# A graph layer on one core: other sizes of the last node blocks, narrower ranges for the last chunks, and row loads every 76 gathers up to near the end

## The chip, the cores and the metric

The kernel runs on one core of a Trainium2 chip. A core has five engines, each with its own queue of instructions: TensorE (PE; loads of weights are listed apart, as PEld), VectorE (DVE), ScalarE (ACT), GpSimd (POOL) and SyncE (SP, which here does nothing but start transfers). The time is that of the device from start to end of the launch, in microseconds (us); lower is better.

## What is computed

One layer of a graph network over 12,500 nodes of 128 features and 200,000 edges. `dst` is sorted, `src` is not.

```python
h = jnp.maximum(_layernorm(x, axis=-1), 0.0)
msgs = h[src]
agg = jax.ops.segment_sum(msgs, dst, num_segments=n)
deg = jax.ops.segment_sum(jnp.ones((src.shape[0],)), dst, num_segments=n)
agg = agg / jnp.maximum(deg, 1.0)[:, None]
g = jax.nn.relu(agg @ Wg + h @ Ws + bg)
g = jnp.tanh(g @ W1 + b1)
g = jnp.tanh(g @ W2 + b2)
out = x + g @ W3 + b3
```

Wg and Ws are 128x128, W1 128x512, W2 512x512, W3 512x128. All is float32.

## The kernel before

**Chunks.** The edges are cut into 1563 chunks of 128 edges. Since `dst` is sorted, a chunk's destinations lie in a short range of nodes: `window(c)` (L97) gives its first node and its width from `WINDOWS` (L49), 144 nodes for most chunks, 88 from chunk 1496, 56 from chunk 1536. A chunk takes one matmul: its 128 source rows are the weights, and a one-hot matrix (edge by node of the range) streams, so that sums per node arise in PSUM, features on the partitions. The one-hots are made by DVE for eight chunks at a time (`onehot`, L349), with a sum over the eight (`cnt`) from which `count` (L379) takes the nodes' degrees.

**Where rows come from.** There are three ways to fetch the 128 source rows of a chunk:

- 80 raw chunks (`raw`, L80) take rows of x before the layer norm, by 80 gathers on POOL during the set-up, and are normed later.
- Most chunks take one gather on POOL from the table `htab` of normed rows in DRAM (`gather`, L297), at most `AHEAD` = 32 gathers ahead of the chunk that is being added.
- The chunks of the list `slow` (L84) are fetched row by row by SP, with 128 transfers of 512 bytes (`row_loads`, L314). Their addresses are loaded in the set-up (`at_i`, one transfer a chunk on ACT's queue; `place`, one DVE instruction). The list begins at chunk `SLOW0` = 160 and then takes a chunk after each `EACH` chunks that are not raw. The rows are loaded in batches of `LOADS` = 16; eight batches, spread over about `EACH` gathers, fill one of two buffers (L637).

**Blocks.** The nodes are cut into blocks (L104): 23 of 512, then 256, 128, 128, 128 and the remaining 84. `reach` lists the chunks whose range touches a block; chunks that touch two blocks are summed into a bank of their own, `edge`, and `merge` (L438) adds that to both. When the last of a block's chunks is added, and two more chunks (`lead`, L648, in the last part), the block is merged and its layers begin: `part0` multiplies by the reciprocal degree (`mT`, DVE), then ws and wg; `part1` to `part3` are the three dense layers, with an ACT step after each product; `part4` turns the result back by TensorE transposes and adds x.

**Order.** TensorE's instructions stand in an order written out by the main loop (L616): chunk by chunk, with steps of the layers in between. From chunk `QUICK` = 1376 on, a small plan of due times (`there`, L642, and `costs`, L493) decides which layer steps go between two chunks. SP's transfers stand in program order as well: loads of own rows (`hb`), of x (`xb`, `xs`), the batches of row loads, and stores of results. POOL does nothing but gathers.

At the end the kernel sums the degrees; if an edge fell outside its range, they don't add up to 200,000, and a second, general way computes all again (`flag`, L674).

Of the kernel before, what the change touches and what calls it, by code (L numbers as in the profile page):

```python
# [31 lines left out]
P = 128  # L32
EPS = 1e-5
CPR = 16
BLK = 512
# [4 lines left out]
STEP = 40  # L40
AHEAD = 32
SLOW0 = 160
EACH = 80
LOADS = 16
LATE = 12
LEAD = 10
QUICK = 1376

WINDOWS = ((0, 144), (1496, 88), (1536, 56))  # L49
W_RAW = 160  # L50
W_MAX = max(W_RAW, *(w for _, w in WINDOWS))

# [6 lines left out]
def windowed(ctx, tc, x, src, dst, Wg, Ws, bg, W1, b1, W2, b2, W3, b3, out, flag):  # L59
    nc = tc.nc  # L60
    N, D = x.shape
# [9 lines left out]
    NCH = -(-E // P)  # L71
# [4 lines left out]
    assert D == P and H % P == 0 and per * E == N * P and RAW0 % GRP == STEP % GRP == 0  # L76
    assert all(c % GRP == 0 for c, _ in WINDOWS) and RAW1 <= WINDOWS[1][0]


    def raw(c):  # L80
        return RAW0 <= c < RAW1 and (c - RAW0) % STEP < GRP


    slow, n = [], 0  # L84
    for c in range(SLOW0, NCH - 100):
        if not raw(c):
            if n == 0:
                slow.append(c)
                n = EACH
            else:  # L90
                n -= 1


    def first(w, span=per):
        return (span - w) // 2

    def window(c):  # L97
        if raw(c):
            return per * (c - c % GRP) + first(W_RAW, per * GRP), W_RAW
        w = [w for c0, w in WINDOWS if c0 <= c][-1]  # L100
        return per * c + first(w), w

    blocks, n = [], 0
    for w in [BLK] * (N // BLK - 1) + [BLK // 2] + [P] * 3:  # L104
        blocks.append((n, w))
        n += w
    blocks.append((n, N - n))

    dram = ctx.enter_context(tc.tile_pool(name="dram", bufs=1, space=bass.MemoryType.DRAM))
    const = ctx.enter_context(tc.tile_pool(name="const", bufs=1))  # L110
# [24 lines left out]
    q_i = const.tile([P, CPR], I32, name="q_i")  # L135
    nc.gpsimd.iota(q_i, pattern=[[per, CPR]], base=first(WINDOWS[0][1]), channel_multiplier=0)

# [47 lines left out]
    with tc.tile_pool(name="setup", bufs=1) as sp, tc.tile_pool(name="ln", bufs=2) as ln:  # L185
# [58 lines left out]
        )  # L244
        for c0, w in WINDOWS[1:]:
            v = low[:, c0:]
# [3 lines left out]
        nc.vector.scalar_tensor_tensor(  # L250
            steps[:, :, :GRP], rdst, float(first(WINDOWS[0][1]) - first(W_RAW, per * GRP)),
            at[:, :, :1].to_broadcast([P, NRAW, GRP]), op0=ALU.add, op1=ALU.subtract,
# [118 lines left out]
    for c in range(NCH):  # L371
        lo, w = window(c)
# [243 lines left out]
    for c in range(NCH):  # L616
# [18 lines left out]
        if not raw(c) and c not in slow:  # L635
            behind += 1
            batch = behind * P // (EACH * LOADS)  # L637
            if behind > SLOW0 - 2 * EACH and batch > (behind - 1) * P // (EACH * LOADS):
                next(loading, 0)
# [366 lines left out]
@with_exitstack  # L1006
def gnn_kernel(ctx: ExitStack, tc: tile.TileContext, *args):
    nc = tc.nc
    keep = ctx.enter_context(tc.tile_pool(name="flags", bufs=1))
    flag = keep.tile([1, 1], I32, name="flag")  # L1010
    with ExitStack() as inner:
        windowed(inner, tc, *args, flag)
    outside = nc.values_load(flag, min_val=0, max_val=P)
    with tc.If(outside > 0):
        with ExitStack() as inner:
            general(inner, tc, *args)
# [31 lines left out]
```

## Time and profile before

| | us |
|---|---|
| median of 3 runs | 1957.18 (1956.88 to 1958.13) |
| the profiled execution, its time | 1961.69 |
| the profiled execution, its span | 1959.5 |
| POOL: 80 raw gathers | 77.4 busy, first part of the span |
| POOL: 1467 gathers from `htab` | 1387.6 busy, started from 104.7 to 1938.6 |
| PE busy | 1393.8 |
| DVE busy | 1068.2 |
| mean granted clock of TensorE | 0.901 |

A page of the profile has the busy time of each engine, the chain of work that ended last (followed back from the last instruction to what released it), and the costliest groups of instructions: source line, engine, operation, what is written from what, count, busy time, mean duration in ns, and the idle time just before them with what ended it. "issue" is time in which an engine waited for nothing that the profile shows. A timeline lists instructions in order; a table by stages has the busy time of each engine in a stretch of the span, and the share of full speed that TensorE's clock was granted in it. TensorE's float32 products appear as two passes each, so "x2" is one matmul. Numbers such as L299 are lines of the kernel before.

### The profile page before, as it was taken

The page shows a single profiled execution, that of the slowest core. Times are in us where ns is not written, and L with a number is a line of the kernel's source. Part 1 is how long each engine was busy: PE and PEld are TensorE (multiplying, and loading weights), DVE is VectorE, ACT ScalarE, POOL GpSimd, SP SyncE. Part 2 cuts the span into 40 slices and gives each one's busy share as a digit, 9 for nine tenths or more (in the row PEclk, how much of TensorE's full clock was granted, in tenths as well). Part 3 has the DMA queues.
Part 4 walks back from the last instruction along what each step waited for, and adds up shares of the span by engine and source line. Part 5 has one row for each costly group of instructions (what it writes and reads, how often), then busy time and mean ns, then how long its engine had stood idle before and what let it go on. Part 6 is the DMA issues. An engine that isn't in the chain of part 4 may idle for free.

```text
span 1959.5 us, 19291 instructions
## 1 busy us (share of the span) xinstructions
PE 1393.8 (71%) x5213; PEld 824.1 (42%) x5213; DVE 1068.2 (55%) x650; ACT 231.8 (12%) x364; POOL 1465.9 (75%) x1555
## 2 busy tenths in 40 slices
PE   0056677777788778877777777777677677778897
PEld 0034344444454445533443434444343333454566
DVE  6974775555667656645545545455454554545430
ACT  1100211011111111010110110110001101101122
POOL 7777777777777777777777777777777777777774
PEclk9999778899989998899989888889889898879697
DMA  7822222222222222222222222222222222222221
GB/s 195 232 69 64 54 64 65 59 70 69 59 65 70 66 74 54 70 70 53 71 59 65 69 53 70 65 59 70 59 65 64 60 70 59 71 69 69 56 61 40
DMA packets 123684, 139.31 MB, mean 71 GB/s; under 512 B 32558, under 2 KB 97978, under 8 KB 123372
## 3 DMA queue, kind: packets, MB, share of 16 engines
q0 software_dynamic: 49504, 101.48, 20.4%
q1 hardware_dynamic: 70870, 33.19, 6.2%
q10 hardware_dynamic: 3192, 3.32, 0.6%
q8 instruction: 43, 0.70, 0.2%
q14 instruction: 75, 0.61, 0.1%
HBM read 125.05 MB, written 12.82 MB: 70 GB/s over the span
## 4 chain that ended last, share of the span: by engine, by line
DMA 36%; issue 28%; PE 26%; POOL 7%; DVE 3%; ACT 0%; SPq 0%; ACTq 0%; POOLq 0%; DVEq 0%
DMA rows<-htab,scol 34%; PE pm L286 13%; PE agg L286 9%; POOL rows L299 7%; PE edge L286 3%; DMA xt<-in_x_dram 2%; PE pt L289 1%; DMA at_i<-in_src_dram 0%; DVE oh L357 0%; DVE agg L176 0%; DVE h L183 0%; DVE agg L172 0%; DVE xt L173 0%; DVE cnt L367 0%; DVE shared L176 0%
## 5 line engine op out<-in xcount | busy, mean ns | idle before, releaser
L299 POOL DMA_INDIRECT rows<-htab,scol x1467 | 1387.6, 946 | 447.5 <-issue 269.3
L286 PE MATMUL agg<-oh,rows 128*128 128x144 f32 (+3 forms) x2096 | 560.2, 365 | 335.2 <-DMA rows<-htab,scol 324.3
L286 PEld LDWEIGHTS agg<-oh,rows 128*128 128x128 f32 x2096 | 381.9, 223 | 714.1 <-DMA rows<-htab,scol 597.5
L286 PE MATMUL pm<-h,w 128*128 128x512 f32 (+3 forms) x1344 | 639.0, 573 | 1.1 <-ACT h L515 0.7
L357 DVE TENSOR_TENSOR oh<-shared,dloc 128x1152 f32<-128x1152 f32 (+2 forms) x186 | 243.9, 1318 | 542.0 <-PE agg L286 330.6
L367 DVE TENSOR_REDUCE cnt<-oh 128x200 bf16<-128x1600 f32 (+2 forms) x186 | 524.3, 2824 | 4.6
L286 PE MATMUL edge<-oh,rows 128*128 128x144 f32 (+2 forms) x838 | 212.2, 346 | 124.3 <-DMA rows<-htab,scol 123.8
L286 PEld LDWEIGHTS edge<-oh,rows 128*128 128x128 f32 x838 | 145.0, 210 | 277.1 <-DMA rows<-htab,scol 242.3
L286 PEld LDWEIGHTS pm<-h,w 128*128 128x128 f32 x1344 | 219.8, 202 | 15.2 <-issue 12.0
L540 ACT ACTIVATE h<-pm,b2c 128x512 f32<-128x512 f32 (+3 forms) x112 | 70.9, 633 | 554.8 <-PE pm L286 554.8
L527 ACT ACTIVATE h<-pm,b1c 128x512 f32<-128x512 f32 (+3 forms) x112 | 70.5, 633 | 237.4 <-PE pm L286 236.9
L142 POOL DMA_INDIRECT raw<-in_x_dram,rsrc x80 | 77.4, 967 | 25.5 <-issue 23.8
L394 DVE RECIPROCAL rd<-rd 128x512 f32<-128x512 f32 (+3 forms) x28 | 81.8, 2920 | 0.0
L564 DVE TENSOR_TENSOR o<-pt,xb 128x512 f32<-128x512 f32 x23 | 15.9, 690 | 95.7 <-PE pt L289 91.9
L508 DVE TENSOR_TENSOR mT<-agg,rd 128x512 f32<-128x512 f32 (+3 forms) x28 | 17.4, 620 | 86.6 <-PE agg L286 86.6
L201 PE MATMUL pm<-ident,idx_f 98*128 98x98 f32 x32 | 6.2, 376 | 64.2 <-DVE idx_f L197 57.8
L392 DVE TENSOR_SCALAR rd<-pm 128x512 f32<-128x512 f32 (+3 forms) x28 | 17.4, 622 | 61.6 <-PE pm L286 61.6
L515 ACT ACTIVATE h<-pm,bgc 128x512 f32<-128x512 f32 (+3 forms) x28 | 17.7, 633 | 271.8 <-PE pm L286 271.8
L472 ACT COPY hT<-pt 128x512 f32<-128x512 f32 (+1 forms) x25 | 14.4, 578 | 258.5 <-PE pt L289 246.9
L286 PE MATMUL pm<-hT,ws 128*128 128x512 f32 (+3 forms) x56 | 41.2, 831 | 0.0
L550 ACT ACTIVATE h<-pm,b3c 128x512 f32<-128x512 f32 (+3 forms) x28 | 17.7, 633 | 181.9 <-PE pm L286 181.9
L289 PE MATMUL pt<-ident,hb 128*128 128x128 f32 x98 | 16.6, 297 | 31.5 <-DMA srows<-htab 31.5
(69 smaller groups left out, 499.1 us busy)
## 6 DMA issues: line engine op xcount, KB each, us to landing
srows<-htab SPq DMA_DIRECT2D x2048, 0.5 KB
rows<-htab,scol POOLq DMA_INDIRECT x1467, 2.5
hb<-htab SPq DMA_DIRECT2D x24, 256.0 KB
xb<-in_x_dram SPq DMA_DIRECT2D x23, 256.0 KB
out_dram<-o SPq DMA_DIRECT2D x23, 256.0 KB
htab<-h SPq DMA_DIRECT2D x6, 896.0 KB
xt<-in_x_dram SPq DMA_DIRECT2D x5, 896.0 KB
raw<-in_x_dram,rsrc POOLq DMA_INDIRECT x80, 3.9
```

The source lines that it names most:

```text
L142: nc.gpsimd.indirect_dma_start(out=t[:, j, :], out_offset=None, in_=x, in_offset=bass.IndirectOffsetOnAxis(ap=rsrc[:, g, j : j + 1], axis=0),)
L286: tc.keep_in_program_order(nc.tensor.matmul(*a, **k))
L289: tc.keep_in_program_order(nc.tensor.transpose(*a, **k))
L299: nc.gpsimd.indirect_dma_start(out=r, out_offset=None, in_=htab, in_offset=bass.IndirectOffsetOnAxis(ap=scol[:, c : c + 1], axis=0),)
L357: nc.vector.tensor_tensor(oh[:, :k, :w], lane[:, None, :w].to_broadcast([P, k, w]), dloc[:, g * GRP : g * GRP + k][:, :, None].to_broadcas ...
L367: nc.vector.tensor_reduce(cnt[:, :n], shifted, AX.X, ALU.add)
L392: nc.vector.tensor_scalar(rd[:, :m], dg[:, :m], 1.0, None, op0=ALU.max)
L394: nc.vector.reciprocal(rd[:, :m], rd[:, :m])
L515: nc.scalar.activation(h0s[b][:, :n], p0[:, :n], AF.Relu, bias=bgc)
L527: nc.scalar.activation(h1s[b][:, m, :n], p1[:, :n], AF.Tanh, bias=b1c[:, m : m + 1])
L540: nc.scalar.activation(h2s[b][:, m, :n], p2[:, :n], AF.Tanh, bias=b2c[:, m : m + 1])
L550: nc.scalar.activation(h3s[b][:, :n], p3[:, :n], AF.Identity, bias=b3c)
```

## The change

Four edits, in one function:

- `EACH` is 76 instead of 80, and `slow` runs to 12 chunks before the end instead of 100.
- `WINDOWS` has a further entry: from chunk 1552 on a range is 40 nodes wide instead of 56.
- The last blocks are 256, 128, 128, 112 and 100 nodes instead of 256, 128, 128, 128 and 84.
- An assertion that the last block has at most 128 nodes.

```diff
-EACH = 80
+EACH = 76
...
-WINDOWS = ((0, 144), (1496, 88), (1536, 56))
+WINDOWS = ((0, 144), (1496, 88), (1536, 56), (1552, 40))
...
     slow, n = [], 0
-    for c in range(SLOW0, NCH - 100):
+    for c in range(SLOW0, NCH - 12):
         if not raw(c):
             if n == 0:
                 slow.append(c)
                 n = EACH
             else:
                 n -= 1
...
     blocks, n = [], 0
-    for w in [BLK] * (N // BLK - 1) + [BLK // 2] + [P] * 3:
+
+    for w in [BLK] * (N // BLK - 1) + [BLK // 2] + [P] * 2 + [P - 16]:
         blocks.append((n, w))
         n += w
     blocks.append((n, N - n))
+    assert 0 < N - n <= P
```

## The prediction

> **What bounds the kernel now.** I read the page's head first, then the chain of waits, the costliest groups, the timeline of the last 25 us, and the stages of busy time.
>
> ```profile
> span 1959.5 us, 19291 instructions
> PE 1393.8 (71%) x5213; PEld 824.1 (42%) x5213; DVE 1068.2 (55%) x650; ACT 231.8 (12%) x364; POOL 1465.9 (75%) x1555
> ...
> DMA 36%; issue 28%; PE 26%; POOL 7%; DVE 3%; ACT 0%; SPq 0%; ACTq 0%; POOLq 0%; DVEq 0%
> ...
> L299 POOL DMA_INDIRECT rows<-htab,scol x1467 | 1387.6, 946 | 447.5 <-issue 269.3
> ```
>
> POOL looks 75% busy, but its idle time is 0.30 us before each of the 1467 gathers: 0.946 + 0.305 = 1.251 us. The waits of POOL agree: none before a gather is over 0.3 us. The gathers start at 104.73 and 1938.59, and 1833.86 / 1466 = 1.251. **POOL is the bound from 104.73 to 1938.59, and never waits**; the chain names the gather's landing ("DMA") and "issue", which are the same thing seen from TensorE. The first gather follows the last raw one (103.48) by that same 1.25 us, so POOL is the bound from the start too: 80 raw gathers lie before it.
>
> What remains is the tail after the last gather (the timeline; columns: start, duration, engine, line, operation):
>
> ```profile
> 1933.61 0.50 PEld L286 LDWEIGHTS agg<-oh,rows 128*128 128x128 f32 x2 [0.53 <-DMA rows<-htab,scol]
> ...
> 1938.59 0.95 POOL L299 DMA_INDIRECT rows<-htab,scol  x1 [0.30 <-POOLq L1014]
> ...
> 1943.61 0.30 PEld L286 LDWEIGHTS agg<-oh,rows 128*128 128x128 f32 x2
> ...
> 1944.06 0.25 DVE L508 TENSOR_TENSOR mT<-agg,rd 128x84 f32<-128x84 f32 x1 [8.78 <-PE agg L286]
> ...
> 1945.84 0.30 PEld L286 LDWEIGHTS pm<-mT,wg 128*128 128x128 f32 x2
> ...
> 1946.57 0.33 PE L289 MATMUL pt<-ident,h 128*128 128x128 f32 x1 [0.27 <-ACT h L550]
> 1946.80 5.79 PE L286 MATMUL pm<-h,w 128*128 128x84 f32 x48
> ...
> 1953.35 0.29 DVE L567 TENSOR_TENSOR o<-pt,xs 84x128 f32<-84x128 f32 x1 [6.12 <-PE pt L289]
> ```
>
> 1933.61 is chunk 1556, the last before block 26 is merged; 1943.61 is chunk 1562, the very last. A gather's rows are usable 2.52 to 2.73 us after its start where TensorE waits for them (1931.09 to 1933.61, say), so chunk 1562 could have run at 1938.59 + 2.58 = 1941.17; it ran 2.44 later, because TensorE was still in block 26's layers. The mean of block 27 was ready at 1944.31, but its weights came at 1945.84: 1.5 us behind block 26 again. From 1953.64 to 1959.5 the last store lands.
>
> **Part 1, row loads (spacing 76, up to near the end).** Counting the list's rule through, slow chunks go from 16 to 18 (the new last ones: 1395, 1472, 1549), gathers from 1467 to 1465. Two gathers at 1.251 us: **-2.50**; the last gather starts at 1936.09, its rows are usable at 1938.67.
> What this adds: SP issues 256 more row DMAs, register moves and 16 loads of `place`. A stretch of row loads (25.12 us for 64) gives 0.39 us a row, so 100 us of SP. Two thirds lie beyond 1680, where SP had no rows. It is hidden: SP waits 574 us for results to store, 228 for `agg` matmuls, out of 1850. For chunk 1549 the last batch is issued at chunk 1463 in SP's order, behind the store of block 21; that goes out by about 1808 (the later of SP's two stores in the stretch from 1772.53), 16 rows are 6 us, so they are there near 1814, and TensorE wants them near 1922. No TensorE wait of before is put down to such rows' landing. Queued behind these batches on SP are loads of `hb` and `xb`; the `hb` load of 1817.79 is used at 1898 (pt at 1897.99), so several us are free there. A slower TensorE pace (1.3% more chunks per gather) cannot stall POOL either: a gather is refused only with 32 buffers full, 40 us behind, and the farthest that a chunk's matmul lies behind its gather in this trace is 19.9 us, at 1707.
> In the set-up ACT issues two more index loads (0.25 to 0.79 us each), DVE does one more `low` update (0.19), and `place` moves behind the last `h` (it now stands in DVE's order after it). ACT and DVE lie beside POOL's raw gathers. The first gather's own wait was cleared at 98.4, 6.3 us before POOL reached it: cost 0 until the set-up slips by more. Both ends: 0 to +1 of loss; I take 0.
>
> **Part 2, sizes of the last blocks (112 and 100 for 128 and 84) and ranges of 40 from chunk 1552.** By the ranges, block 26 now needs chunks up to 1551 instead of 1554, and is merged two chunks later, at 1553 instead of 1556. Chunk 1553's rows are usable 9 gathers before chunk 1562's: 1938.67 - 11.26 = 1927.41. So block 26's chain starts 1933.61 - 1927.41 = 6.20 us earlier.
> From there to the end of block 26's last transpose TensorE took 1946.90 - 1933.61 = 13.3 us, with 6 chunks and 2 matmuls of block 27 between. In the new order of TensorE it has 8 chunks and three small count matmuls (0.34) between: the same number of pieces, 13.6 us. Chunk 1562 stands right behind: 1941.0 at this clock, at the earliest 1938.67, by its rows. So it moves **2.6 to 4.9** us forward, the 2.50 of part 1 among it.
> Behind it nothing of block 26 is left: the 1.5 us wait of block 27's weights goes. Late next is block 27's own chain, 1946.80 on. It is 100 columns instead of 84, but its matmuls are bound by weight loads: results leave ACT each 0.89 us for 8 passes at 84 columns, and 8 passes and a chunk (0.22) took 1.11 at 128, so 0.11 a pass in both. The ACT steps on its path grow by some 0.015 us each (0.33 at 84, 0.37 at 128), four of them and the drain: +0.1. Sum: **-1.4**.
> The narrower ranges save nothing on TensorE (0.33 us at 56 columns, 0.31 at 36), and cost two clears on DVE (0.27), which idles 11 us and 5.5 us in that stretch. That the range is too narrow, which would call the second way of computing, is excluded by the inputs: the drawn destinations stay 14 nodes inside it.
>
> **The clock decides between the ends.** Stages of the tail (length, busy PE, PEld, DVE, ACT, POOL, granted clock, DMA):
>
> ```profile
> 1911.33:1914.74 3.41, 1.79 (x13) 1.44 (x12) 0.58 (x2) 0.27 (x1) 2.57 (x3) 1.00 0.32 79
> 1914.74:1918.15 3.41, 2.16 (x9) 1.77 (x9) 0.00 (x0) 0.37 (x1) 2.72 (x3) 0.50 0.26 63
> ...
> 1924.98:1928.39 3.41, 2.62 (x25) 2.29 (x23) 1.63 (x4) 0.73 (x2) 2.69 (x3) 1.00 0.22 58
> 1928.39:1931.81 3.42, 1.28 (x6) 0.89 (x6) 0.00 (x0) 0.23 (x1) 2.62 (x3) 0.99 0.29 77
> 1931.81:1935.22 3.41, 2.39 (x12) 2.26 (x13) 1.41 (x6) 0.01 (x1) 2.50 (x4) 0.50 0.15 38
> 1935.22:1938.63 3.41, 3.26 (x15) 3.08 (x15) 0.06 (x1) 1.10 (x3) 2.50 (x4) 0.50 0.24 60
> 1938.63:1942.05 3.42, 3.42 (x19) 3.42 (x18) 0.00 (x0) 1.10 (x3) 0.90 (x1) 0.51 0.19 46
> ```
>
> A stretch of 3.41 us with 1.28 or 1.79 us busy is followed by half clock; one with 2.62 is not; it returns after a full one. At half clock ten passes take 2.25 us, at full 1.2. [...] By the row, a stretch half empty suffices, and block 26 runs as slow as before: -2.6 - 1.4 = -4.0. The hole of before (1928.4 to 1931.8) had nothing but chunks; from 1927.4 it now holds the merge, two first-layer matmuls and the counts, about 2.9 us busy, but the stretch just before it may be the empty one, and where the windows fall is chance. I take the row with a part of the gain: **-4.8**. Against the profiled execution, 1961.69: 1956.9. The median of the runs shown is 4.5 lower, 1957.18, so 1952.4; a few us of tail and of POOL steps are the same in both.
>
> **Rivals.**
> *The tail gives it back.* TensorE, earlier with block 26, waits for chunks 1560 to 1562; the clock falls there, and block 27's 48 passes run two windows at half clock: +3.4 on -6.3, -2.9, so 1954.3. For it: the new tail has no other work to fill those waits. Against: block 26's layers fill most of 1930 to 1938.
> *The gathers alone.* Tail as before, or a set-up slipped past its cover: -2.5 to 0, 1954.7 to 1957.2. For it: SP and ACT share waits in the set-up that the trace shows only in one order. Against: 6.3 us of cover.
> *Slower: SP late with chunk 1549.* TensorE runs in order, so late rows there hold the 13 chunks and both blocks behind it, with nothing to hide them. It decides once SP is more than 1922 - 1814 = 108 us late; for +4 it must be 117 late (4 + 4.8 to win back): 1961. For it: SP is held up to 63.4 us by one store. Against: it would need two such waits in a row, and SP is idle more than half the time.
>
> **Numbers.** A run of this kernel tells 0.2% (3.9 us, below 1953.3) from no change. Forecast 0.62, own range 1950 to 1954; tail given back 0.2; gathers alone 0.1; slower 0.08. Faster: most of the forecast's and a little of the first rival's, 0.62; within: 0.30; slower 0.08. Range 1949.6 (-6.3 and a full-clock chance of 1.3 more) to 1955.6.
>
> **What would show it.** 1465 gathers 1.251 apart, first at 104.7, last at 1936.1; chunk 1562's weights between 1938.7 and 1941; its mean's matmul within 1 us behind it; last DVE step near 1949. Wrong if the first gather is late, if a wait over 0.3 us stands before any gather, if TensorE waits for `srows`, or if the last 48 passes take over 7 us.

## The result, and the profile after

| | before | after |
|---|---|---|
| median of 20 runs each, us | 1957.08 (1956.07 to 1958.13) | 1953.22 (1950.54 to 1957.15) |
| profiled execution, its time / its span | 1961.69 / 1959.5 | 1956.59 / 1954.8 |

The medians lie 3.86 us apart. The means, 1957.00 and 1954.03, lie 2.97 apart, and the ratio, which weighs all runs, says the same: 0.9985 with an interval of 0.9978 to 0.9992, or 1.6 to 4.3 us. The times of after spread wider, which makes the difference between the two figures: 14 of the 20 lie between 1950.54 and 1954.56, six between 1956.59 and 1957.15.

Both profiled executions are long ones. That of after is one of the six. That of before, 1961.69, lies above all 68 times of before shown here and below (1955.91 to 1958.44).

Of the page of after, the head, the chain and the group of the gathers:

```profile
span 1954.8 us, 19826 instructions
PE 1389.3 (71%) x5212; PEld 820.3 (42%) x5212; DVE 1068.4 (55%) x651; ACT 231.7 (12%) x364; POOL 1463.5 (75%) x1553
...
DMA 34%; issue 29%; PE 25%; POOL 11%; ACT 0%; SPq 0%; DVE 0%; POOLq 0%; ACTq 0%
...
L301 POOL DMA_INDIRECT rows<-htab,scol x1465 | 1385.3, 946 | 446.9 <-issue 270.9
```

Lines are two higher than before (L299 is now L301). There are 1465 gathers of the same 946 ns, 446.9 / 1465 = 0.305 us of idle before each. The waits of POOL in after (for what, us in total, times, longest) show that nothing else was added:

```profile
POOL rows L301 <- issue: 270.9, 888, 0.3
POOL rows L301 <- PE agg L288: 73.2, 240, 0.3
```

No wait before a gather is over 0.3 us. The gathers start from 104.94 to 1935.88. The tail in the timeline of after:

```profile
1927.25 0.30 PEld L288 LDWEIGHTS agg<-oh,rows 128*128 128x128 f32 x2 [0.28 <-DMA rows<-htab,scol]
...
1935.88 0.95 POOL L301 DMA_INDIRECT rows<-htab,scol  x1 [0.30 <-DMA rows<-htab,scol]
...
1938.79 0.30 PEld L288 LDWEIGHTS agg<-oh,rows 128*128 128x128 f32 x2 [0.22 <-DMA rows<-htab,scol]
...
1939.54 0.30 PEld L288 LDWEIGHTS pm<-mT,wg 128*128 128x128 f32 x2 [0.23 <-DVE mT L510]
...
1940.44 7.48 PE L288 MATMUL pm<-h,w 128*128 128x100 f32 x48 [0.43 <-ACT h L517]
...
1948.71 0.29 DVE L569 TENSOR_TENSOR o<-pt,xs 100x128 f32<-100x128 f32 x1 [9.22 <-PE pt L291]
```

1927.25 is chunk 1553, behind which block 26 is merged; 1938.79 is chunk 1562, which now waits for nothing but its own rows ("DMA rows"); 1939.54 are block 27's first weights, 0.75 us behind and held by the mean alone. Before, they stood 2.23 us behind. One line is worse: the 48 passes took 7.48 us, where before 84 columns took 5.79. The stages (length, PE, PEld, DVE, ACT, POOL, granted clock, DMA share, GB/s) say why:

```profile
1934.83:1938.25 3.42, 2.67 (x23) 2.39 (x21) 0.00 (x0) 0.93 (x3) 1.69 (x2) 1.00 0.24 60
1938.25:1941.66 3.41, 2.69 (x15) 2.02 (x16) 0.55 (x2) 1.19 (x5) 0.00 (x0) 0.99 0.07 19
1941.66:1945.07 3.41, 3.41 (x18) 3.41 (x17) 0.00 (x0) 0.79 (x3) 0.00 (x0) 0.51 0.00 0
1945.07:1948.49 3.42, 2.98 (x27) 2.80 (x25) 0.00 (x0) 1.38 (x4) 0.00 (x0) 1.00 0.00 0
```

One stretch, 1941.66 to 1945.07, runs at half clock, in the middle of the last block's layers, where nothing lies beside them.

Between the two profiled executions the span fell by 4.7 us. The pieces add up: the last gather -2.71 (1938.59 to 1935.88), chunk 1562 behind the last gather -2.11 (5.02 to 2.91), from chunk 1562 to the end of the last DVE step +0.18 (10.03 to 10.21), from there to the end of the span -0.06 (5.86 to 5.80).

### The profile page after: what moved, and what is told of

Same layout as the page of the kernel before. It is cut to its first block, busy times and chain, and to the rows that moved or that the text cites. A ratio compares the mean times of both kernels' runs of the same rounds, so it can differ in the third digit from the quotient of the medians.

```text
span 1954.8 us, 19826 instructions
## 1 busy us (share of the span) xinstructions
PE 1389.3 (71%) x5212; PEld 820.3 (42%) x5212; DVE 1068.4 (55%) x651; ACT 231.7 (12%) x364; POOL 1463.5 (75%) x1553
## 4 chain that ended last, share of the span: by engine, by line
DMA 34%; issue 29%; PE 25%; POOL 11%; ACT 0%; SPq 0%; DVE 0%; POOLq 0%; ACTq 0%
DMA rows<-htab,scol 34%; PE pm L288 13%; PE agg L288 8%; POOL rows L301 7%; POOL raw L144 4%; PE edge L288 3%; PE pt L291 1%; SPq L297 0%; DVE oh L359 0%; ACT h L517 0%; DMA rsrc<-in_src_dram 0%; ACT h L552 0%; SPq L322 0%; POOLq L301 0%; DMA srows<-htab 0%
## 5 line engine op out<-in xcount | busy, mean ns | idle before, releaser
L301 POOL DMA_INDIRECT rows<-htab,scol x1465 | 1385.3, 946 | 446.9 <-issue 270.9
L288 PE MATMUL pm<-h,w 128*128 128x512 f32 (+4 forms) x1344 | 628.1, 564 | 1.6 <-ACT h L517 1.3
L542 ACT ACTIVATE h<-pm,b2c 128x512 f32<-128x512 f32 (+4 forms) x112 | 70.9, 633 | 554.3 <-PE pm L288 554.3
L529 ACT ACTIVATE h<-pm,b1c 128x512 f32<-128x512 f32 (+4 forms) x112 | 70.2, 633 | 238.9 <-PE pm L288 238.5
L396 DVE RECIPROCAL rd<-rd 128x512 f32<-128x512 f32 (+4 forms) x28 | 81.8, 2920 | 0.0
L510 DVE TENSOR_TENSOR mT<-agg,rd 128x512 f32<-128x512 f32 (+4 forms) x28 | 17.4, 620 | 79.2 <-PE agg L288 79.1
L517 ACT ACTIVATE h<-pm,bgc 128x512 f32<-128x512 f32 (+4 forms) x28 | 17.7, 633 | 281.2 <-PE pm L288 281.2
L288 PE MATMUL pm<-hT,ws 128*128 128x512 f32 (+4 forms) x56 | 41.7, 841 | 0.0
L291 PE MATMUL pt<-ident,hb 128*128 128x128 f32 x98 | 16.3, 292 | 33.1 <-DMA srows<-htab 32.4
L394 DVE TENSOR_SCALAR rd<-pm 128x512 f32<-128x512 f32 (+4 forms) x28 | 17.4, 620 | 39.4 <-PE pm L288 37.5
L552 ACT ACTIVATE h<-pm,b3c 128x512 f32<-128x512 f32 (+4 forms) x28 | 17.7, 633 | 175.5 <-PE pm L288 175.5
```

Of the source, the lines that this page charges most:

```text
L288: tc.keep_in_program_order(nc.tensor.matmul(*a, **k))
L291: tc.keep_in_program_order(nc.tensor.transpose(*a, **k))
L301: nc.gpsimd.indirect_dma_start(out=r, out_offset=None, in_=htab, in_offset=bass.IndirectOffsetOnAxis(ap=scol[:, c : c + 1], axis=0),)
L394: nc.vector.tensor_scalar(rd[:, :m], dg[:, :m], 1.0, None, op0=ALU.max)
L396: nc.vector.reciprocal(rd[:, :m], rd[:, :m])
L517: nc.scalar.activation(h0s[b][:, :n], p0[:, :n], AF.Relu, bias=bgc)
```

## The experiments

The first four kernels ran together; before took 1956.96 (1955.91 to 1958.44, 48 runs) beside them.

### Row loads alone

```diff
-WINDOWS = ((0, 144), (1496, 88), (1536, 56), (1552, 40))
+WINDOWS = ((0, 144), (1496, 88), (1536, 56))
...
-    for w in [BLK] * (N // BLK - 1) + [BLK // 2] + [P] * 2 + [P - 16]:
+    for w in [BLK] * (N // BLK - 1) + [BLK // 2] + [P] * 3:
```

> Only the row loads of the change (spacing 76, up to near the end); blocks and ranges as before. Theory 1 (two terms that add up): two gathers fewer at 1.251 us, so 2.5 us under the kernel before (1954.6 by the median), with a tail behind the last gather as long as before. Theory 2 (all of the gain is the gathers, the tail gives its part back): the same 2.5 to 4 us, as much as the whole change. Theory 3 (the second cluster of times of the changed kernel, 1956.6 to 1957.2, comes from SP's row loads in the last part): its times fall into two clusters too.

Measured: 1954.17 (1953.13 to 1955.13, 21 runs), ratio 0.9986 (0.9979 to 0.9992), so -2.8. The two gathers are worth what they cost on POOL within the interval, and SP's 256 more rows cost nothing that shows. The range is as narrow as that of before and has no second cluster, so the wide spread of after does not come from the row loads. Its timeline still has the old order at the end:

```profile
1932.67 0.94 POOL L299 DMA_INDIRECT rows<-htab,scol  x1 [0.30 <-POOLq L1014]
...
1939.04 0.30 PEld L286 LDWEIGHTS pm<-mT,wg 128*128 128x128 f32 x2
...
1946.54 0.29 DVE L567 TENSOR_TENSOR o<-pt,xs 84x128 f32<-84x128 f32 x1 [6.12 <-PE pt L289]
```

Block 27's weights at 1939.04 have no idle time before them: TensorE comes straight from block 26.

### Blocks and ranges alone

```diff
-EACH = 76
+EACH = 80
...
-    for c in range(SLOW0, NCH - 12):
+    for c in range(SLOW0, NCH - 100):
```

> Only the sizes of the last blocks and the narrower ranges; row loads as before, 1467 gathers. Theory 1: the tail behind the last gather is 1.5 to 2.5 us shorter, 1954.6 to 1955.6. Theory 2: no change, 1957 within 0.5. If the changed kernel's two clusters come from where the 3.41 us windows of the clock fall in the tail, this kernel shows the same two clusters, some 4 us apart, and rows_only does not.

Measured: 1956.23 (1954.22 to 1960.39, 13 runs), ratio 0.9999 (0.9990 to 1.0007): -0.7 by the medians, not told from nothing. Its times spread over 6 us, as those of after do, where before beside it spreads over 2.5: the spread comes with the new sizes and ranges, though not in two clusters. Its profiled execution, 1954.52, is one of its shortest, and has the tail as designed:

```profile
1934.69 0.94 POOL L299 DMA_INDIRECT rows<-htab,scol  x1 [0.30 <-PE pm L286]
...
1939.04 0.30 PEld L286 LDWEIGHTS pm<-mT,wg 128*128 128x128 f32 x2 [0.30 <-DVE mT L508]
...
1939.94 5.85 PE L286 MATMUL pm<-h,w 128*128 128x100 f32 x48 [0.43 <-ACT h L515]
...
1946.57 0.29 DVE L567 TENSOR_TENSOR o<-pt,xs 100x128 f32<-100x128 f32 x1 [7.58 <-PE pt L289]
```

The 48 passes at 100 columns take 5.85 us at full clock against 5.79 at 84, so the wider block costs next to nothing there, and from the last gather to the end of the last DVE step it takes 12.17 us where before took 15.05. That is 2.9 us in one trace, and 0.7 by the medians.

### The changed kernel once more

No edit. 

> The changed kernel again, to see another profiled execution of it. All theories: two clusters of times, most near 1952.5 and some near 1957. If the clock makes them, a profiled execution of the low cluster has no stretch at half clock in the last 48 passes (5.8 us for them), and one of the high cluster has one or two (7.5 to 9.2 us). If the set-up or the pace of the gathers makes them, the last gather starts up to 4 us apart in the two.

Measured: 1952.63 (1949.99 to 1956.53, 10 runs), ratio 0.9979 (0.9969 to 0.9988). The profiled execution is 1952.84, and its tail kept the clock in the last block:

```profile
1932.38 0.94 POOL L301 DMA_INDIRECT rows<-htab,scol  x1 [0.30 <-DMA rows<-htab,scol]
...
1938.80 5.85 PE L288 MATMUL pm<-h,w 128*128 128x100 f32 x48 [0.43 <-ACT h L517]
```

It had 6.8 us of half clock earlier, from 1926.9, in block 26; chunk 1562 therefore ran 4.65 us behind the last gather. Compared with after's trace, the signs of both explanations came true: the 48 passes took 5.85 us instead of 7.48, and the last gather started 3.50 us earlier.

The five tails beside each other (us; the pace is the time from one gather's start to the next; the last column has the half clock that stands last before the end of the 48 passes):

| profiled execution | pace | last gather to chunk 1562 | chunk 1562 to last DVE step's end | sum | half clock from, for |
|---|---|---|---|---|---|
| before | 1.2509 | 5.02 | 10.03 | 15.05 | 1931.8, 10.2 |
| row loads alone | 1.2485 | 4.13 | 10.03 | 14.16 | 1927.3, 6.8 |
| blocks and ranges alone | 1.2484 | 3.47 | 8.70 | 12.17 | 1926.3, 6.8 |
| after | 1.2506 | 2.91 | 10.21 | 13.12 | 1941.7, 3.4 |
| changed kernel once more | 1.2484 | 4.65 | 8.70 | 13.35 | 1926.9, 6.8 |

The new sizes make the fourth column 1.33 shorter at full clock (10.03 to 8.70), twice alike; one half-clock stretch there takes 1.5 of it back. The third column moves between 2.91 and 4.65 with the same code, by where the half-clock stretch falls. The two kernels with the new tail and the pace 1.2484 against row loads alone, whose tail is the old one at that pace, give 0.8 to 2.0 us in the sum, one trace each. Against the trace of before it would be 1.7 to 2.9: that trace had 10.2 us of half clock in its tail and is the longest of the five.

The second column holds a surprise of its own: executions differ by 2.4 us in a thousand gathers. Busy time of one gather was 945.9 and 945.6 ns in the traces of before and after, 943.5 in the other three, with the same 0.305 idle. Over 1465 gathers that is 3.1 to 3.5 us, as much as the change is worth.

### A warmer clock

88-column products with no use are put into TensorE's expected waits from chunk 1500 on, and two behind the last block's `wg`.

```diff
+    def warm(n):
+        for _ in range(n):
+            pe.matmul(shared[:, 260:348], ident, ident[:, :88], start=True, stop=True, skip_group_check=True)
...
+        if b == len(blocks) - 1:
+            warm(2)
...
+            if c >= 1500:
+                warm(int(0.7 * (there - now) / 0.22))
```

> The changed kernel with small matmuls whose result nobody reads, in the waits of TensorE from chunk 1500 on and two behind the last block's first layer. They add work and take none away. If half clock in the tail makes the high cluster: the cluster near 1957 goes, and the times lie at 1951 to 1953.5. If it does not: the same two clusters, or all times later by the added work (0.3 to 1 us).

Measured: 1954.39 (1950.63 to 1956.94, 15 runs), ratio 0.9984 (0.9976 to 0.9992). The spread stayed, and so did the half clock. Stages of this kernel, columns as above:

```profile
1920.88:1924.29 3.41, 2.17 (x18) 2.04 (x18) 0.00 (x0) 0.23 (x1) 2.62 (x3) 1.00 0.32 82
1924.29:1927.71 3.42, 3.42 (x19) 3.42 (x18) 0.28 (x1) 0.00 (x0) 2.50 (x4) 0.51 0.14 38
1927.71:1931.12 3.41, 3.41 (x20) 3.41 (x19) 1.28 (x5) 1.77 (x5) 2.50 (x4) 0.50 0.22 58
1931.12:1934.53 3.41, 3.41 (x18) 3.41 (x17) 0.00 (x0) 0.35 (x1) 1.82 (x2) 0.50 0.24 60
```

The fillers left the stretch before the drop 2.17 of 3.41 busy. In this trace chunk 1562 ran 6.69 us behind the last gather, the most of all, and the last 48 passes kept the clock (5.85 us). So the kernel can't say what a clock that never drops would give. It does show that three wholly busy stretches (3.42, 3.41 and 3.41) passed before the clock came back.

In this case's traces the number of streamed columns goes with the clock that follows more closely than busy time does. Add up, for each stretch of 3.41 us, the columns of the TensorE passes in it (100 for a pass on 128x100; a pass that crosses an edge is shared by time). The six traces so far have 3,056 such stretches. Those with fewer than 1,520 columns were followed by half clock and those with more by full clock, whatever the clock was before, with 33 exceptions. In the eight traces of the next section, which had no part in finding the 1,520, there are 41 exceptions in 5,024. The best cuts by busy time (54% at full clock, 86% at half) leave 170 exceptions in the 3,056. This is a count over the traces of these runs, made afterwards; no kernel was run to test it, and what the hardware itself counts is not shown. The stretches of this document:

| kernel, from | clock | busy PE | columns | clock next |
|---|---|---|---|---|
| before, 1924.98 | full | 2.62 | 2063 | full |
| before, 1928.39 | full | 1.28 | 336 | half |
| after, 1934.83 | full | 2.67 | 1957 | full |
| after, 1938.25 | full | 2.69 | 1297 | half |
| changed kernel once more, 1923.50 | full | 2.60 | 1291 | half |
| this kernel, 1920.88 | full | 2.17 | 1254 | half |
| this kernel, 1924.29 | half | 3.42 | 1188 | half |
| this kernel, 1927.71 | half | 3.41 | 1595 | half (an exception) |
| this kernel, 1931.12 | half | 3.41 | 1538 | full |

Passes of 40 columns, as the last chunks have, fill time and add little to the count: in this kernel's trace, at full clock, a chunk's two (80 columns) took 0.33 us and ten passes of 112 columns (1,120) 1.35.

### Stronger warming, more row loads, no second way

The first four kernels ran on chip 4. The other eight, in three sets on chips 9, 0 and 3, were slow throughout: before took 2306.89, 2304.03 and 2302.38 there, 18% more. Why is not known. POOL's gathers are as short as ever in these sets but no longer the bound. The group of the gathers and one of POOL's waits, in the kernel without the second way (below):

```profile
L301 POOL DMA_INDIRECT rows<-htab,scol x1465 | 1385.6, 946 | 774.9 <-issue 308.4
...
POOL rows L301 <- PE agg L288: 127.7, 127, 13.0
```

The idle time has risen from 447 to 775, and POOL now waits for TensorE, up to 13.0 us at once. Row loads follow each other on SP at 0.71 us in the median (register move and transfer), where it was 0.32 in the first trace of before. What a gather or a tail is worth where POOL is the bound can't be read here.

**Nine 512-column products**, from chunk 1552 on in TensorE's expected waits and behind `wg` of each of the last two blocks, three times:

```diff
+        if b >= len(blocks) - 2:
+            fill(1)
...
+            if c >= 1552:
+                fill(int((there - now) / 0.43))
```

> The changed kernel with nine 512-column matmuls whose result nobody reads: in TensorE's waits from chunk 1552 on and behind wg of the last two blocks. They need no wait for DVE, unlike those of warm, and stream 512 columns each, where those streamed 88. If half clock in the tail spreads the times of the changed kernel: no stretch at half clock from chunk 1552 to the end, times within about 2 us of each other near 1951. If something else spreads them: the same spread of 6 us, with up to 1 us of work added.

> The same kernel as warm2, since that set ran where every kernel, the one before too, took 2307 us and POOL waited for TensorE. Where the kernel before takes 1957: if half clock in the tail spreads the changed kernel's times (1950 to 1957), no half-clock stretch from chunk 1552 to the end and times within 2 us of each other near 1951. If something else spreads them: the same spread, with up to 1 us added.

> The changed kernel with nine 512-column matmuls in TensorE's waits from chunk 1552 on and behind wg of the last two blocks; the third set of it. Where the kernel before takes 1957: if half clock in the tail spreads the changed kernel's times, times within 2 us of each other near 1951 and no half-clock stretch from chunk 1552 to the last transpose; if something else does, the same spread of 6 us. Where it takes 2304: 4 to 5 us over it, as in the set before.

Measured: ratios 1.0043 (1.0027 to 1.0060), 1.0026 (1.0012 to 1.0040) and 1.0050 (1.0032 to 1.0068). Where POOL waits for TensorE already (127.7 us in the waits above), the kernel with the added products took 0.3 to 0.5% longer than before; whether they would narrow the times near 1953 stays open.

**Still more row loads**, three times (`EACH` 64, 21 chunks, 1462 gathers):

```diff
-EACH = 76
+EACH = 64
```

> The changed kernel with a row-loaded chunk after each 64 gathers instead of 76: 21 such chunks, 1462 gathers, three fewer than the changed kernel. If POOL's gathers are the price, with SP still hidden: 3 x 1.25 = 3.75 us under the changed kernel, 1949 by the median. If the row loads take part of it back (SP, the transfers' share of the memory): less than 2 us, and a wait over 0.3 us before some gathers, or TensorE waits for srows.

> The same kernel as each64, where the kernel before takes 1957: 1462 gathers. If POOL's gathers are the price and SP stays hidden: 3.75 us under the changed kernel's 1952.6 to 1953.2, so near 1949. If the row loads take a part back: less than 2 us under it, and waits over 0.3 us before some gathers.

> A row-loaded chunk after each 64 gathers instead of 76, 1462 gathers; the third set of it. Where the kernel before takes 1957 and POOL never waits: 3.75 us under the changed kernel, so near 1949, with all waits before gathers at 0.3 us. Where it takes 2304 and POOL waits for TensorE: 70 us or more over the kernel before, as in the two sets so far.

Measured: ratios 1.0381 (1.0361 to 1.0401), 1.0309 (1.0285 to 1.0334) and 1.0325 (1.0300 to 1.0351), 71 to 88 us more. The waits of TensorE and of SP in the third (for what, us in total, times, longest):

```profile
PE pt L291 <- DMA hb<-htab: 237.3, 13, 23.1
...
SPq L297 <- DMA srows<-htab: 56.2, 112, 1.4
...
SPq L297 <- DVE o L566: 30.8, 3, 11.1
```

In the kernel with `EACH` 76 and no second way, TensorE's wait is one of 30.7 us at the start. It ran in another set, on chip 9; the first `EACH` 64 run of that same set has 318.8 us in 17 waits.

```profile
PE pt L291 <- DMA hb<-htab: 30.7, 1, 30.7
```

It is not the rows that are late but what is queued behind them on SP: the blocks' own rows, `hb`. In the changed kernel on chip 4 SP still waited 335.7 us for results to store, in 18 waits; the `EACH` 76 kernel of chip 9 has 114.9 left, and this one 30.8. So here row loads were free while SP had waits to put them in. Whether 21 such chunks would pay where before takes 1957 us was not measured.

**Without the second way.**

```diff
-    outside = nc.values_load(flag, min_val=0, max_val=P)
-    with tc.If(outside > 0):
-        with ExitStack() as inner:
-            general(inner, tc, *args)
```

> The changed kernel without its second way of computing, and so without the branch at the end: it leaves out the reading of the flag, the branch and the code that is jumped over. If the last store's landing sets the end, as the prediction had it: no change beyond 0.5 us. If TensorE's branch does (4.2 to 4.3 us in both profiled executions, from the last transpose on): 1.5 to 4 us under the changed kernel.

**Blocks and ranges alone, again**, beside it: 

> Only the sizes of the last blocks and the narrower ranges, once more, for a second profiled execution and more times. If the clock spreads this kernel's times (1954.2 to 1960.4 before): the time from the last gather to the last DVE step, 12.2 us in its first profiled execution, moves with the half-clock stretches in the tail: about 11.5 without any, up to 17 with 10 us of them. If the pace of the gathers does: the same 12 us, and a pace other than 1.2484.

Measured: 2307.09, ratio 1.0003 (0.9991 to 1.0016), and 2309.81, ratio 1.0009 (0.9998 to 1.0020): no difference that shows. The changed kernel itself was not in that set, and the times of one kernel spread over some 13 us in it, so the 1.5 to 4 us in question can't be told by time. What can be read is the end, in one trace each. From the timelines, first without the second way (span 2306.9), then with it (span 2303.4):

```profile
2303.97 0.29 DVE L569 TENSOR_TENSOR o<-pt,xs 100x128 f32<-100x128 f32 x1 [7.59 <-PE pt L291]
2304.29 0.31 SPq L297 DMA_DIRECT2D out_dram<-o  x1
```

```profile
2297.44 0.29 DVE L567 TENSOR_TENSOR o<-pt,xs 100x128 f32<-100x128 f32 x1 [7.59 <-PE pt L289]
2297.76 0.34 SPq L295 DMA_DIRECT2D out_dram<-o  x1
```

From the last DVE step's end to the end of the span: 2.64 us and 5.67. With the second way, its branch sets the end and not the store: 3.0 us more. In the traces of before and after TensorE's branch over it takes 4.24 and 4.34 us, in the other three of the table 3.88 to 4.18.

## The prediction against the runs

The forecast, 1952.4, was 0.8 below the measured 1953.22. The direction is right, and the larger part of the mechanism, the two gathers, is shown by a run of its own. That the sum came out so close is in part luck: the gathers gave a little more than forecast and the tail less. By its steps:

- **POOL bounds the kernel; two gathers are -2.50.** Right: 1465 gathers, first 104.94 (104.7 said), last 1935.88 (1936.1 said), no wait over 0.3; -2.8 when done alone.
- **SP's 256 rows and the set-up hidden.** Right. Chunk 1549's rows were issued by 1820 (1814 said) and used at 1925. The first gather came 0.2 us later. One reading was wrong without harm: the page of before does put a TensorE wait down to row loads, 31.5 us, but it is one in the set-up, which ends at 101.9 and is 32.4 us long in after.
- **Block 26 two chunks earlier; chunk 1562 2.6 to 4.9 earlier.** Right in the trace: chunk 1553 at 1927.25 (1927.41 said), chunk 1562 at 1938.79, 4.82 earlier. Other executions show its lag behind the last gather at up to 4.65 us, close to before's 5.02.
- **Block 27's own chain, -1.4.** Right at full clock: -1.33. In after's trace a half-clock stretch fell into it and made it +0.18. The prediction had named over 7 us for the last 48 passes as a sign against it; they took 7.48. That is the rival "the tail gives it back" in half its size, one stretch instead of two, at 1.5 us.
- **The term that was mis-sized is the tail: -2.3 of the -4.8.** By the medians it is -0.7 by itself, -1.1 on top of the row loads' -2.8 (3.86 - 2.8), or -1.5 within one set (1954.17 to 1952.63). By the means it is smaller: -0.4 by itself, -0.2 for after against row loads alone (ratios 0.9985 and 0.9986), -1.4 for the changed kernel once more (95% interval -2.6 to -0.2), and -0.6 for these 30 runs together (-1.4 to 0.2). So the times make some gain likely, but they do not exclude the rival "the gathers alone". In the traces the new tail is shorter, by 0.8 to 2.0 us against row loads alone. The prediction sized its gain on the trace of before, whose tail was the longest of the five; no second trace of before is there to say how typical it is.
- **Why the gain does not reach the times.** Shown: the kernels with the new tail spread over 6 us, where row loads alone spread over 2, and with the same code the half clock falls into block 26, where it delays chunk 1562, or into block 27, where it costs 1.5 us. Not shown: why six of after's times lie near 1957. The one of them that was traced has both that stretch (1.5 us) and the longer gathers (2.1 ns each more than 943.5: 3.1 us), and the other five have no trace. That the new tail has to do with the gathers' pace is no more than a suspicion: before had the longer gathers in its own profile, though none of its 68 times is near that one.
- **The rule for the clock failed.** "2.62 of 3.41 busy keeps it" was taken from one pair of rows. In after, 2.67 kept it and 2.69 did not; by the count of columns these are 1957 and 1297, on both sides of 1,520. What holds of it is that no idle stretch was needed: all the stretches before a drop in the table above had work in them, 1.28 to 2.69 us. The range and the first rival start from -6.3, a tail at full clock throughout with chunk 1562 2.58 us behind the last gather and block 27's chain 1.4 shorter; no run shows it. The runs gave 2.91 behind with the chain 0.18 longer, and 3.47 and 4.65 behind with it 1.33 shorter, each with 3.4 to 6.8 us of half clock in the tail.
- **"From 1953.64 the last store lands."** Wrong: it is TensorE's branch that ends last. It is in both kernels, and so cost the sum nothing.

None of the versions that were run was shown to be faster than the changed kernel.

## What to carry to other kernels

Where one queue bounded the kernel and never waited, an instruction taken off it was worth its full interval (-2.50 forecast, -2.8 measured for two). Here the queue that took the work over was free only while it still had waits to fill (335.7 us of waits for results at `EACH` 76 on chip 4, 30.8 at 64 on chip 3), and the first victim was another load queued behind, `hb`, for which TensorE then waited 237.3 us. A gain in a tail that half clock can touch needs a width of its own in the range: here single traces gave 0.8 to 2.9 us, the medians 0.7 to 1.5, the means 0.2 to 1.4. Before a tail is compared between two traces, the pace of the bounding queue is to be compared, and whether the traced execution is a typical one. When a stretch looks busy enough to keep the clock, its columns are worth counting beside its busy time: in the six traces the best cuts by busy time left 170 exceptions, the cut by columns 33.

## Not expected of the hardware

- The same gather took 943.5 ns in three profiled executions and 945.9 and 945.6 in those of before and after: 3.1 to 3.5 us in 1465.
- Fewer than 1,520 streamed columns in a stretch of 3.41 us were followed by half clock, more by full clock, in all but 74 of 8,080 stretches of 14 traces. In the kernel with 88-column fillers TensorE was wholly busy (3.42 of 3.41 us) with 1,188 columns, and the clock stayed at half; it came back after three wholly busy stretches there, and after one (3.42 and 3.41 busy) in the tails of before and of after.
- TensorE's branch past the second way, whose code isn't executed, took 3.9 to 4.3 us at the end (five traces, 4.24 in that of before); without it the end of the span was 3.0 us shorter (2.64 against 5.67).
- In three sets, on three chips, the kernel before took 18% longer; the traces of these sets have SP's row loads 0.6 to 0.7 us apart in the median instead of 0.32, and a granted clock of 0.77 to 0.80 instead of 0.90 to 0.92.
